# First-stage values in two small tiles by turns, attention's tiles laid out around the first stage, and slots' zeros written in 64 pieces during attention

## The chip, the cores and the metric

The kernel runs on one core of a Trainium2 chip. The metric is the device time of one execution in microseconds (us), here the median of a few runs. TensorE is called PE in the profile (its weight loads PEld), VectorE DVE, ScalarE ACT, GpSimd POOL and SyncE SP; "SPq" and "ACTq" are the sequencers that issue DMAs. All work is in fp32.

## The reference, cut to what matters

Two layers work on an image tensor of 4 x 384 x 32 x 32. What is computed around the change is the first half of layer 0, and where layer 1 needs zeros:

```
x = x + conv0(ln_c(x))          # conv0 is attention with relative positions
    qkv = xt @ w_qkv            # 4096 tokens x 384 -> 3 x 384, 8 heads of 48
    attn = q k^T * s + sk[dy, dx] + sq[dy, dx];  softmax over 1024 keys
    out  = attn v + (attn summed by offset) table_v;  out @ w_proj + b_proj
t = t + ffn0(ln(t))
x = x + conv1(ln_c(x))          # depthwise convolutions, 7 x 7
t = t + moe(ln(t))              # 4 experts, the 2 best of each token
```

For the experts the kernel sorts token rows into an array of slots in device memory, `xs_d`: 4 experts x 4096 slots of 384 numbers, 25.2 MB. Slots that no token fills must hold zeros, so the whole array is zeroed before the tokens' rows are scattered into it.

## The kernel before, in words

The program has three phases, one after the other in the source: `qkv_phase` (the first stage), `attention_phase` and `rest_phase`. A scheduler orders the instructions of each engine; instructions that are marked `keep_in_program_order` (`pin`, and the helpers `mm`, `dma`, `bulk`, lines 223 to 235) keep their written order among themselves. Tiles of on-chip memory are taken from pools (named groups of buffers). When a pool is closed, its bytes are free for the next pools, and an instruction that writes a tile over freed bytes first waits until the earlier users of those bytes are done.

**First stage** (lines 133 to 202). The 4096 tokens come in 8 blocks of 512, `t` = 0 to 7. `load(t)` fetches the block `xt` on SP's queue; line 160 fetches the weights `wq`. `token_stats` (lines 78 to 98) transposes the block on PE with the matrix `ident` (line 87) and takes mean and variance on DVE; `center` (lines 121 to 130) subtracts the mean over input rows from the weights, once, with the matmuls of line 128. `ident` itself is made at the very start by `make_identity` (line 1501; a memset and an affine select on POOL, shown as masks.py:197 and masks.py:199). For each block PE makes the per-token scale (line 117), six products of q and k rows (36 matmuls, line 175), the next block's statistics and four products of value rows (24 matmuls, line 186). DVE scales each q or k product into one of four buffers `qk_sb` (line 179), and POOL's queue writes it to device memory, `qk_d` (line 180). ACT scales the value products into `va` (line 189), one tile for all 8 blocks, zeroed in one POOL memset (line 147); POOL's queue writes each block's part to `v_d` (line 194). In blocks 2 to 5 POOL's queue also writes the zeros of `xs_d`, two transfers of 3072 KB per block, from a tile `zero` of one row (lines 198 to 202).

**Attention** (lines 205 to 651). Small loads come first: the tables `tab`, q and k of head 0 as `kq` (lines 273 to 285), keys `kk`. For each of 8 heads `prepare` (lines 298 to 324) makes two tables of position terms: 32 pairs of matmuls `tabq_ps` and `tabk_ps`; DVE transposes each `tabk_ps` into the tile `b2` (line 318), ACT copies each `tabq_ps` into `st` (line 322), and SP's queue writes `st` to device memory, `sd`. Then come 32 rows `y` of the image (lines 565 to 639), for all 4 images at once. The row loop is a software pipeline written out by hand. For row `y` it issues, on SP's queue, `queries` for two rows ahead (line 568, even `y`), `fetch(blk[y + 3])` (line 570: a load of `s1` out of `sd`, 240 KB, then POOL additions at line 353 that make the tile `bias`), and one piece of the head's value table `tvw` (`next(pieces)`, line 574, 192 KB). DVE adds `bias` to the scores (line 381) two rows ahead, ACT takes exponentials (line 391), PE transposes (line 410) and, every fourth row, multiplies with the values `vb` (line 440, `av_ps`). From `y` = 19 on ACT's queue loads the next head's `kq` (line 576). All waits run through buffers: three of `s1`, three of `bias`, two of `qs`, two score buffers `sc_ps`.

**Layout.** The pools of the first stage and those of attention start at the same byte of each partition, behind the pool `held`. Within a pool tiles lie in the order in which they are written down. The first stage has `va` (65,536 bytes per partition), `zero` (1,536), `wq` (13,824), then three `xt` (18,432), the small tiles, two `scale` (4,096), `s_dg` (2,048) and four `qk_sb` (8,192). Attention's pool `a_fixed` has `b2` (61,440), three pairs of `arow` and `extra` (18,432), two `den` (256), then `vb` (8,192), `aT` (16,384), `a1t` (32,768), `tvs` (1,024), `tvw` (24,576); the working tiles (`st`, `bias`, `s1`, `oT`, `qs`) lie behind these, past the first stage's last byte.

**Rest** (from line 894): projection, feed-forward, convolution, gates, scatter into `xs_d` (line 1205), experts. Its first scatter runs 1763.6 us into the span.

Of the kernel before, what the change touches and what calls it, by code (L numbers as in the profile page):

```python
# [11 lines left out]
F32 = mybir.dt.float32  # L12
# [6 lines left out]
P = 128  # L19
B, C, IMG = 4, 384, 32  # L20
# [3 lines left out]
HEADS, HD = 8, C // 8  # L24
# [4 lines left out]
NBLK = N // P  # L29
PADR = 6  # L30
AROWS = IMG + 2 * PADR
YB = 4
YT = 16
XT = 8
VW = 64
# [3 lines left out]
NEXP = 4  # L39
TOK = 512  # L40
# [6 lines left out]
CAP = B * N  # L47
# [23 lines left out]
def bcast(ap, dim, n):  # L71

    dims = [list(d) for d in ap.ap]
    dims[dim] = [0, n]
    return bass.AP(ap.tensor, ap.offset, dims)
# [25 lines left out]
def result(steps):  # L101

    while True:
        try:
            next(steps)
        except StopIteration as end:
            return end.value
# [13 lines left out]
def center(nc, psum, tag, one, w):  # L121

    n = w.shape[2]
    for c in range(0, n, C):
        part = w[:, :, c : min(c + C, n)]
        ps = psum.tile([P, part.shape[2]], F32, tag=tag, name="sum_ps")
        for k in range(KC):
            nc.tensor.matmul(ps, one, part[:, k, :], start=(k == 0), stop=(k == KC - 1))
        for k in range(KC):
            nc.vector.scalar_tensor_tensor(part[:, k, :], ps, -1.0 / C, part[:, k, :], ALU.mult, ALU.add)  # L130


def qkv_phase(tc, cst, x, w_qkv, qk_d, v_d, xs_d):

    nc = tc.nc
    one, ident = cst["one"], cst["ident"]
    with ExitStack() as es:  # L140
        wp = es.enter_context(tc.tile_pool(name="q_w", bufs=1))
        work = es.enter_context(tc.tile_pool(name="q_work", bufs=2))
        ev = es.enter_context(tc.tile_pool(name="q_ev", bufs=4))
        psum = es.enter_context(tc.tile_pool(name="q_ps", bufs=3, space=PSUM))
        psmm = es.enter_context(tc.tile_pool(name="q_mm", bufs=4, space=PSUM))
        va = wp.tile([P, HEADS, B * NBLK, VW], F32, name="va")
        nc.gpsimd.memset(va, 0.0)
        zero = wp.tile([P, 1, C], F32, name="zero")
        nc.gpsimd.memset(zero, 0.0)
        wq = wp.tile([P, KC, 3 * C], F32, name="wq")  # L150
        xts = {}

        def load(t):
            b, n0 = divmod(t * TOK, N)
            xts[t] = work.tile([P, KC, TOK], F32, tag="xt", name="xt", bufs=3)
            nc.sync.dma_start(xts[t], x[b, :, n0 : n0 + TOK].rearrange("(k p) n -> p k n", p=P))

        load(0)
        for k in range(KC):
            nc.sync.dma_start(wq[:, k, :], w_qkv[k * P : (k + 1) * P, :])  # L160
        stats = result(token_stats(nc, (work, psum, "st"), ident, xts[0], cst["eps6"]))
        center(nc, psum, "st", one, wq)
        for t in range(NT // TOK):
            b, n0 = divmod(t * TOK, N)
            xt = xts.pop(t)
            _, rstd = stats
            ps = to_partitions(nc, (work, psum, "st"), ident, one, rstd)
            scale = work.tile([P, TOK], F32, tag="scale", name="scale")
            nc.scalar.copy(scale, ps)
            if t + 1 < NT // TOK:  # L170
                load(t + 1)
            for m in range(2 * KC):
                ps = psmm.tile([P, TOK], F32, tag="mm", name="qk_ps")
                for k in range(KC):
                    nc.tensor.matmul(
                        ps, wq[:, k, m * P : (m + 1) * P], xt[:, k, :], start=(k == 0), stop=(k == KC - 1)
                    )
                sb = ev.tile([P, TOK], F32, tag="qk", name="qk_sb")
                nc.vector.tensor_tensor(sb, ps, scale, ALU.mult)
                nc.gpsimd.dma_start(qk_d[m * P : (m + 1) * P, t * TOK : (t + 1) * TOK], sb)  # L180
            if t + 1 < NT // TOK:
                stats = result(token_stats(nc, (work, psum, "st"), ident, xts[t + 1], cst["eps6"]))
            for j in range(TOK // P):
                ps = psmm.tile([P, TOK], F32, tag="mm", name="v_ps")
                for k in range(KC):
                    nc.tensor.matmul(
                        ps[:, :C], xt[:, k, j * P : (j + 1) * P], wq[:, k, 2 * C :], start=(k == 0), stop=(k == KC - 1)
                    )
                nc.scalar.activation(
                    va[:, :, t * (TOK // P) + j, :HD], ps[:, :C].rearrange("p (h d) -> p h d", d=HD),  # L190
                    AF.Copy, scale=rstd[:, j, :],
                )
            w = NBLK // 2 * VW
            nc.gpsimd.dma_start(
                v_d.rearrange("h p n -> p h n")[:, :, t * w : (t + 1) * w],
                va[:, :, t * NBLK // 2 : (t + 1) * NBLK // 2, :].rearrange("p h c d -> p h (c d)"),
            )
            if 2 <= t < 2 + NEXP:
                rows = xs_d[(t - 2) * CAP : (t - 1) * CAP].rearrange("(n p) c -> p n c", p=P)
                n = rows.shape[1] // 2  # L200
                for r in (rows[:, :n], rows[:, n:]):
                    tc.keep_in_program_order(nc.gpsimd.dma_start(r, bcast(zero, 1, r.shape[1])))


def attention_phase(tc, cst, held, tabs, tv, qk_d, v_d, ao_d, heads):

# [12 lines left out]
    nc = tc.nc  # L221
# [15 lines left out]
    with ExitStack() as es:  # L237
        dram = es.enter_context(tc.tile_pool(name="a_dram", bufs=2, space=DRAM))
        fixed = es.enter_context(tc.tile_pool(name="a_fixed", bufs=1))
# [4 lines left out]
        ps_o = es.enter_context(tc.tile_pool(name="a_ps_o", bufs=1, space=PSUM))  # L244

        ident = cst["ident"]
        b2 = fixed.tile([P, SPAN, IMG, IMG], F32, name="b2")

        NA = 3
        arow, extra = [], []  # L250
        for i in range(NA):
            a = fixed.tile([P, AROWS, IMG], F32, name=f"arow{i}")
            nc.gpsimd.memset(a, 0.0)
            arow.append(a)
            x = fixed.tile([P, 4, IMG], F32, name=f"extra{i}")
            nc.gpsimd.memset(x, 0.0)
            extra.append(x)
        den = []
        for i in range(2):
            d = fixed.tile([P, IMG], F32, name=f"den{i}")  # L260
# [2 lines left out]


        kq, kk, tab = held
        vb = fixed.tile([P, B, NBLK, VW], F32, name="vb")
        aT = fixed.tile([P, NBLK, YB, P], F32, name="aT")
        a1t = fixed.tile([P, 4, IMG, YT, B], F32, name="a1t")
        tvs = fixed.tile([64 + HD, B // 2, YT, XT], F32, name="tvs")
        nc.gpsimd.memset(tvs, 0.0)  # L270
        tvw = fixed.tile([P, 4, IMG, HD], F32, name="tvw")

        def load_tables(h, bulk=bulk):
            for lo, i, r0 in ((64, 0, h * HD), (0, 1, C + h * HD)):
# [246 lines left out]
                yield  # L521


        batch, o = None, None

        def new_head(h):
            sd = dram.tile([P, IMG, SPAN * IMG], F32, tag="sd", name="sd")
# [8 lines left out]
        for n, h in enumerate(heads):  # L536
# [28 lines left out]
            for y in range(IMG):  # L565
                s, r = blk[y], y % YT
# [5 lines left out]
                    add_aside(batch[1], 3)  # L572
                if y:
                    next(pieces, None)
                if y >= YT + 3:
                    next(loads, None)
                if batch and r in (3, 7):
# [917 lines left out]
@with_exitstack  # L1495
def metaformer_kernel(ctx: ExitStack, tc: tile.TileContext, ins, out):
    nc = tc.nc
    cp = ctx.enter_context(tc.tile_pool(name="const", bufs=1))
    dram = ctx.enter_context(tc.tile_pool(name="scratch", bufs=1, space=DRAM))
    ident = cp.tile([P, P], F32, name="ident")  # L1500
    make_identity(nc, ident)
    one = cp.tile([P, P], F32, name="one")
    nc.vector.memset(one, 1.0)
    cst = {"ident": ident, "one": one}
    for name, v in (("eps5", 1e-5), ("eps6", 1e-6)):
        t = cp.tile([P, 1], F32, name=name)
        nc.vector.memset(t, v)
        cst[name] = t
    qk_d = dram.tile([2 * C, NT], F32, name="qk_d")
    v_d = dram.tile([HEADS, P, B * NBLK * VW], F32, name="v_d")  # L1510
    ao_d = [dram.tile([C, B, YT * IMG], F32, name=f"ao_d{i}") for i in range(2)]
    x2_d = dram.tile([C, NT], F32, name="x2_d")
    xs_d = dram.tile([NEXP * CAP, C], F32, name="xs_d")
    y_d = dram.tile([ALL * BLK, C], F32, name="y_d")

    with tc.tile_pool(name="held", bufs=1) as pool:
        held = [
            pool.tile([64 + HD, *n], F32, name=name)
            for name, n in (("kq", [NT]), ("kk", [B, N // 2]), ("tab", [SPAN, ZW]))
        ]  # L1520
        qkv_phase(tc, cst, ins["x"], ins["w_qkv"], qk_d, v_d, xs_d)
        attention_phase(tc, cst, held, ins["tabs"], ins["tv"], qk_d, v_d, ao_d, list(range(HEADS)))
    rest_phase(tc, cst, ins["x"], ao_d, ins, xs_d, y_d, x2_d, out)


# [69 lines left out]
```

## Time and profile before

| What | Value |
|---|---|
| runs | 3087.72 us, median of 3 (3082.57 to 3088.3) |
| profiled execution | 3092.57 us |
| its span, first to last instruction | 3090.6 us |
| mean granted PE clock in it | 0.976 of full |
| PE busy | 2929.9 us (95%) |
| first position table of head 0 (`tabq_ps`) starts | 237.46 us |
| last PE instruction of attention ends | 1507.8 us |
| transfers `xs_d<-zero`, 8 of 3072 KB, issued | 102.7 to 205.6 us |

A waits line reads: the engine and its instruction that stood idle, what ended the wait, the sum in us, the number of times, the longest. A timeline line reads: start in us, duration in us, engine, line, operation, out<-in, shape, count, and in brackets the engine's idle time before it and what ended it. A windows line gives, for a stretch of the span, each engine's busy us and instructions, the granted PE clock (PEclk), the share of the 16 DMA engines that were busy and the GB/s that they moved.

### The profile page before, as it was taken

What the parts mean: (1) busy time and instruction counts of PE and PEld (TensorE: products, weight loads), DVE (VectorE), ACT (ScalarE), POOL (GpSimd) and SP (SyncE); (2) the same over time, 40 slices, a digit from 0 to 9 for tenths busy, and PEclk for the clock granted to TensorE, in tenths of its full rate; (3) what the DMA queues carried; (4) which work ended last, traced back from release to release, by engine and by line L of the source; (5) the groups of instructions that cost most, each with busy time, mean ns of one, the idle gap of its engine ahead of it and who ended that gap; (6) DMA issues with size and microseconds to landing.
All of it is one profiled execution on the core that took longest, in us unless ns stands there. A gap on an engine that the chain in (4) does not pass through costs nothing.

```text
span 3090.6 us, 63376 instructions
## 1 busy us (share of the span) xinstructions
PE 2929.9 (95%) x25391; PEld 2020.6 (65%) x25391; DVE 1956.6 (63%) x3575; ACT 1370.8 (44%) x2833; POOL 1170.7 (38%) x1132
## 2 busy tenths in 40 slices
PE   8997999999999999999899789999999989999996
PEld 4544676777677677776533347776577867777775
DVE  2226787878787877777568869999899640001101
ACT  1104666666767666666322232333342243233332
POOL 3223747473747473737400122252124231124412
PEclk9998999999999999999999879999999999999998
DMA  3796565656565656564500314734243065366742
GB/s 123 259 320 212 130 203 131 206 132 203 134 202 134 200 131 196 136 199 128 186 21 34 128 31 156 274 136 154 75 175 132 26 229 215 134 227 250 263 180 72
DMA packets 262791, 500.55 MB, mean 162 GB/s; under 512 B 134736, under 2 KB 186832, under 8 KB 254816
## 3 DMA queue, kind: packets, MB, share of 16 engines
q1 hardware_dynamic: 169168, 247.12, 26.0%
q0 software_dynamic: 43424, 227.84, 20.0%
q10 hardware_dynamic: 49904, 21.53, 3.6%
q8 instruction: 200, 3.28, 0.5%
q14 instruction: 95, 0.78, 0.1%
HBM read 543.58 MB, written 152.37 MB: 225 GB/s over the span
## 4 chain that ended last, share of the span: by engine, by line
PE 67%; DVE 13%; issue 11%; POOL 4%; DMA 3%; ACT 2%; another core or an unknown queue 0%; SPq 0%; POOLq 0%; DVEq 0%; ACTq 0%
PE e_ps L1301 12%; PE y_ps L1279 12%; DVE xb L1089 8%; PE t_ps L410 7%; PE av_ps L227 7%; PE sc_ps L227 7%; PE tabq_ps L227 5%; PE a_ps L420 3%; PE tv_ps L227 2%; PE proj_ps L977 2%; PE tabk_ps L227 1%; PE tap_ps L1137 1%; DVE extra L402 1%; PE f_ps L1012 1%; PE o_ps L1016 1%
## 5 line engine op out<-in xcount | busy, mean ns | idle before, releaser
L1301 PEld LDWEIGHTS e_ps<-xT,w 128*128 128x128 f32 x4824 | 656.5, 193 | 217.7 <-issue 14.6
L353 POOL TENSOR_TENSOR bias<-b,s 128x416 f32<-128x416 f32 (+24 forms) x656 | 659.2, 1042 | 178.1 <-DMA s<-sd 157.5
L1301 PE MATMUL e_ps<-xT,w 128*128 128x128 f32 x4824 | 670.6, 277 | 14.1 <-DVE xb L1030 5.0
L1279 PE MATMUL y_ps<-w,eh 128*128 128x384 f32 x1608 | 651.9, 490 | 17.2 <-ACT eh L1304 14.8
L1089 DVE SCALAR_TENSOR_TENSOR xb<-img,pack,xb 128x1024 f32<-128x1024 f32 (+1 forms) x539 | 634.7, 1241 | 0.0
L1304 ACT ACTIVATE eh<-e_ps,w 128x128 f32<-128x128 f32 x804 | 292.9, 367 | 725.3 <-PE e_ps L1301 669.5
L1269 POOL DMA_INDIRECT w<-in_w,row x134 | 171.4, 1279 | 749.7 <-PE y_ps L1279 301.4
L402 DVE TENSOR_REDUCE extra<-arow 128x32 f32<-128x32 f32 (+24 forms) x768 | 381.3, 555 | 9.4 <-ACT arow L391 5.7
L381 DVE CUSTOM_DVE_ANT_0 arow<-sc_ps,bias 128x1024 f32<-128x1024 f32 x256 | 312.5, 1221 | 107.1 <-issue 55.5
L410 PEld LDWEIGHTS t_ps<-ident,arow 128*128 128x128 f32 x2048 | 221.2, 142 | 175.9 <-ACT aT L411 100.6
L391 ACT ACTIVATE arow<-arow,nm 128x1024 f32<-128x1024 f32 x256 | 302.4, 1181 | 70.8 <-DVE nm L381 70.8
L411 ACT COPY aT<-t_ps 128x512 f32<-128x512 f32 x512 | 278.6, 603 | 95.3 <-PE t_ps L410 95.0
L410 PE MATMUL t_ps<-ident,arow 128*128 128x128 f32 x2048 | 283.2, 282 | 17.1 <-ACT arow L391 17.0
L1282 DVE TENSOR_TENSOR yo<-y_ps,w 128x384 f32<-128x384 f32 x67 | 37.0, 553 | 396.0 <-PE y_ps L1279 387.8
L227 PE MATMUL sc_ps<-kk,qs 48*32 48x512 f32 x4096 | 279.2, 608 | 7.7 <-DVE nm L381 6.7
L1279 PEld LDWEIGHTS y_ps<-w,eh 128*128 128x128 f32 x1608 | 248.3, 193 | 31.9 <-ACT eh L1304 19.4
L227 PEld LDWEIGHTS av_ps<-aT,vb 128*64 128x64 f32 x4096 | 222.3, 137 | 52.0 <-ACT aT L411 40.4
L227 PE MATMUL av_ps<-aT,vb 128*64 128x128 f32 x4096 | 237.7, 274 | 0.0
L318 DVE STREAM_TRANSPOSE b<-tabk_ps 128x480 f32<-128x480 f32 x256 | 218.4, 983 | 23.5 <-PE tabk_ps L227 22.2
L227 PE MATMUL tabk_ps<-tab,kq 48*128 48x480 f32 x512 | 223.0, 582 | 6.1 <-DVE b L318 6.1
L227 PE MATMUL tabq_ps<-tab,kq 48*128 48x480 f32 x512 | 220.1, 579 | 2.1 <-ACT aT L411 1.4
L322 ACT COPY st<-tabq_ps 128x480 f32<-128x480 f32 x256 | 142.3, 560 | 71.0 <-PE tabk_ps L227 45.0
(211 smaller groups left out, 3163.4 us busy)
## 6 DMA issues: line engine op xcount, KB each, us to landing
sd<-st SPq DMA_DIRECT2D x128, 480.0 KB
s<-sd SPq DMA_DIRECT2D x256, 240.0 KB
xs_d<-zero POOLq DMA_DIRECT2D x8, 3072.0 KB
tvw<-in_tv SPq DMA_DIRECT2D x120, 192.0 KB
y_d<-yo SPq DMA_DIRECT2D x67, 192.0 KB
qk_d<-qk_sb POOLq DMA_DIRECT2D x48, 256.0 KB
qs<-qk_d SPq DMA_DIRECT2D x256, 48.0 KB
kq<-qk_d ACTq DMA_DIRECT2D x56, 192.0 KB
```

The lines of the kernel that those rows point to most:

```text
L227: ins = nc.tensor.matmul(*args, **kw)
L318: turn = nc.vector.transpose(b2.rearrange("p e y x -> p x (e y)")[:, i + j], ps[:, j, : SPAN * IMG])
L353: nc.gpsimd.tensor_tensor(bias[:, y0:y1, :], bass.AP(b2.tensor, b2.offset + (e * IMG + y0) * IMG, [list(b2.ap[0]), [(step * IMG + 1) * IMG ...
L381: nc.vector.tensor_tensor_reduce(s["flat"], ps.rearrange("p h n -> p (h n)"), s["bias"].rearrange("p y x -> p (y x)"), -SCALE, BIG, ALU.ad ...
L391: nc.scalar.activation(s["flat"], s["flat"], AF.Exp, bias=s["nm"], scale=-1.0, accum_out=dn[:, y % YT : y % YT + 1])
L402: pin(nc.vector.tensor_reduce(ex[:, i, :], a[:, p0:p1, :].rearrange("p y x -> p x y"), AX.X, ALU.add))
L410: pin(nc.tensor.transpose(pt[:, j, :], s["flat"][:, k0 : k0 + P], ident))
L411: pin(nc.scalar.copy(aT[:, 4 * g : 4 * g + 4, s["y"] % YB, :], pt))
L1089: ins_ = nc.vector.scalar_tensor_tensor(acc[:, k, y0:y1], img[:, k, dy + y0 : dy + y1, dx : dx + IMG], w7[:, k, dy, dx : dx + 1], acc[:, k ...
L1279: nc.tensor.matmul(py, hs, w[:, o : o + C], start=(ff == 0), stop=(ff == NF - 1))
L1301: nc.tensor.matmul(ph, w[:, o : o + P], xT[k][:, c, :], start=(c == 0), stop=(c == KC - 1))
L1304: nc.scalar.activation(hs, ph, AF.Gelu, bias=w[:, o : o + 1])
```

## The change

- `va` of the first stage becomes two tiles `va0` and `va1` of 8,192 bytes per partition, one block each, used by turns (`vas[t % 2]`). They are zeroed by DVE, not POOL.
- The tile `zero` and the writes of zeros into `xs_d` leave the first stage.
- In `attention_phase` the tiles `vb`, `aT`, `a1t` and `tvw` are written down first, ahead of `b2`; so they take the first 81,920 bytes, and `b2`, `arow`, `extra`, `den` and `tvs` lie behind them. A tile `zero` (1,536 bytes, POOL memset) joins them.
- A generator `clear` issues one write of 256 rows of zeros (384 KB) per step on SP's queue, pinned in order; the row loop steps it at `y` = 6, 9, 12, 15, 18, 21, 24 and 27 of each head, after that row's `fetch` and `tvw` piece and ahead of ACT's load for that row. 8 steps by 8 heads make the 64 pieces.

```
-def qkv_phase(tc, cst, x, w_qkv, qk_d, v_d, xs_d):
+def qkv_phase(tc, cst, x, w_qkv, qk_d, v_d):
...
-        va = wp.tile([P, HEADS, B * NBLK, VW], F32, name="va")
-        nc.gpsimd.memset(va, 0.0)
-        zero = wp.tile([P, 1, C], F32, name="zero")
-        nc.gpsimd.memset(zero, 0.0)
+        vas = [wp.tile([P, HEADS, TOK // P, VW], F32, name=f"va{i}") for i in range(2)]
+        for va in vas:
+            nc.vector.memset(va, 0.0)
...
                 nc.scalar.activation(
-                    va[:, :, t * (TOK // P) + j, :HD], ps[:, :C].rearrange("p (h d) -> p h d", d=HD),
+                    vas[t % 2][:, :, j, :HD], ps[:, :C].rearrange("p (h d) -> p h d", d=HD),
...
-                va[:, :, t * NBLK // 2 : (t + 1) * NBLK // 2, :].rearrange("p h c d -> p h (c d)"),
+                vas[t % 2].rearrange("p h c d -> p h (c d)"),
             )
-            if 2 <= t < 2 + NEXP:
-                rows = xs_d[(t - 2) * CAP : (t - 1) * CAP].rearrange("(n p) c -> p n c", p=P)
-                n = rows.shape[1] // 2
-                for r in (rows[:, :n], rows[:, n:]):
-                    tc.keep_in_program_order(nc.gpsimd.dma_start(r, bcast(zero, 1, r.shape[1])))
...
-def attention_phase(tc, cst, held, tabs, tv, qk_d, v_d, ao_d, heads):
+def attention_phase(tc, cst, held, tabs, tv, qk_d, v_d, ao_d, xs_d, heads):
...
         ident = cst["ident"]
+        vb = fixed.tile([P, B, NBLK, VW], F32, name="vb")
+        aT = fixed.tile([P, NBLK, YB, P], F32, name="aT")
+        a1t = fixed.tile([P, 4, IMG, YT, B], F32, name="a1t")
+        tvw = fixed.tile([P, 4, IMG, HD], F32, name="tvw")
         b2 = fixed.tile([P, SPAN, IMG, IMG], F32, name="b2")
...
+        zero = fixed.tile([P, 1, C], F32, name="zero")
+        nc.gpsimd.memset(zero, 0.0)
...
-        vb = fixed.tile([P, B, NBLK, VW], F32, name="vb")
-        aT = fixed.tile([P, NBLK, YB, P], F32, name="aT")
-        a1t = fixed.tile([P, 4, IMG, YT, B], F32, name="a1t")
         tvs = fixed.tile([64 + HD, B // 2, YT, XT], F32, name="tvs")
         nc.gpsimd.memset(tvs, 0.0)
-        tvw = fixed.tile([P, 4, IMG, HD], F32, name="tvw")
...
+        def clear():
+
+            rows = 2 * P
+            for n0 in range(0, NEXP * CAP, rows):
+                dma(
+                    xs_d[n0 : n0 + rows].rearrange("(n p) c -> p n c", p=P), bcast(zero, 1, rows // P),
+                )
+                yield
+
         batch, o = None, None
+        cleared = clear()
...
                 if y:
                     next(pieces, None)
+                if 6 <= y < 30 and y % 3 == 0:
+                    next(cleared)
                 if y >= YT + 3:
                     next(loads, None)
```

More of the change, by code (lines that the diff above doesn't have):

```diff
@@ L1520, in metaformer_kernel @@
         ]
-        qkv_phase(tc, cst, ins["x"], ins["w_qkv"], qk_d, v_d, xs_d)
-        attention_phase(tc, cst, held, ins["tabs"], ins["tv"], qk_d, v_d, ao_d, list(range(HEADS)))
+        qkv_phase(tc, cst, ins["x"], ins["w_qkv"], qk_d, v_d)
+        attention_phase(tc, cst, held, ins["tabs"], ins["tv"], qk_d, v_d, ao_d, xs_d, list(range(HEADS)))
     rest_phase(tc, cst, ins["x"], ao_d, ins, xs_d, y_d, x2_d, out)
```

## The prediction

> **What bounds the kernel now.** I read the page's busy times, then the waits and the timeline of the first stage, then the boundary to attention, then the waits of attention's rows.
>
> ```profile
> PE 2929.9 (95%) x25391; PEld 2020.6 (65%) x25391; DVE 1956.6 (63%) x3575; ACT 1370.8 (44%) x2833; POOL 1170.7 (38%) x1132
> ```
>
> PE is the bound nearly everywhere, so a gain can only come from stretches in which PE stands still or is slowed. The change touches three of them.
>
> The start (timeline; start, duration, engine):
>
> ```profile
> 0.88 13.76 POOL L147 MEMSET va<- 128x16384 f32 x1
> 3.99 0.49 SPq L232 DMA_DIRECT2D tab<-in_tabs  x1
> 14.68 0.28 POOL masks.py:199 TENSOR_SCALAR_AFFINE_SELECT ident<-ident 128x128 f32<-128x128 f32 x1
> ...
> 15.02 2.82 PE L87 MATMUL row_ps<-ident,xt 128*128 128x128 f32 x12 [15.02 <-POOL ident masks.py:199]
> ```
>
> The memset of `va` runs on POOL between the two steps that make `ident`; PE's first instruction waits for `ident`, not for data.
>
> The middle (PE's timeline at line 117, once per block, and the waits of 0 to 240 us):
>
> ```profile
> 100.76 1.02 PE L117 MATMUL all_ps<-s_dg,one 128*128 128x512 f32 x2
> ...
> 126.12 1.02 PE L117 MATMUL all_ps<-s_dg,one 128*128 128x512 f32 x2
> ...
> 151.85 1.02 PE L117 MATMUL all_ps<-s_dg,one 128*128 128x512 f32 x2
> ...
> 184.02 1.02 PE L117 MATMUL all_ps<-s_dg,one 128*128 128x512 f32 x2
> ...
> 210.44 1.02 PE L117 MATMUL all_ps<-s_dg,one 128*128 128x512 f32 x2
> ```
> ```profile
> DVE qk_sb L179 <- DMA qk_d<-qk_sb: 58.7, 10, 14.5
> ...
> PE qk_ps L175 <- DVE qk_sb L179: 7.0, 3, 4.3
> ```
>
> Blocks take 25.36 us each until the zeros come; then 25.73, 32.17 and 26.42. DVE finds its four `qk_sb` still being written out, and PE finds no free bank.
>
> The boundary (timeline):
>
> ```profile
> 237.69 0.90 POOL L194 DMA_DIRECT2D v_d<-va  x1 [7.09 <-ACT va L189]
> ...
> 246.05 0.13 DVE L261 MEMSET den<- 128x32 f32 x2 [16.28 <-DMA kk<-qk_d]
> 246.05 1.27 POOL L253 MEMSET arow<- 128x1408 f32 x1 [7.46 <-DMA sd<-st]
> 246.09 3.44 DVE L318 STREAM_TRANSPOSE b<-tabk_ps 128x480 f32<-128x480 f32 x4
> ```
>
> DVE and POOL start at the same moment, on tiles that lie over the first stage's bytes. The named releasers are only the last in time; what ends here is the last `v_d<-va`, whose packets stop at 244.66 in the trace's packet records. `den` lies over `wq` alone (bytes 79,872 on, by the sizes), whose last reader, PE, was done at 236.8; yet it waits as long, so the freed stretch is handed over whole. `st`, past those bytes, was written from 238.73.
>
> In the rows there is little for a delay to hide behind or to free:
>
> ```profile
> PE t_ps L410 <- ACT arow L391: 8.5, 13, 2.2
> PE sc_ps L227 <- DVE nm L381: 6.7, 10, 1.0
> ```
>
> These are PE's two longest waits of 300 to 1500 us. Starts of the value products (line 440) are 13.80 or 13.81 us apart in all eight heads: PE sets the pace of the rows.
>
> **What the Trainium skill says.** (1) "DMA: Bandwidth & Descriptors", section Queues, rings and completion order: each DMA engine takes descriptors in ring order within a queue and goes round between queues. The trace agrees: `qk_d` writes, behind 3072 KB of zeros in POOL's queue, hold DVE up to 14.5 us. It says too where the zeros go: ahead of fetches in SP's ring. (2) "TensorE: Matmul & The Clock Gate", section What's actually happening: after some 3.4 us of idling the array falls to half clock until it has been busy again. The trace agrees: after the gap at 242 to 248 us `tabk_ps` takes 1.17 us, else 0.56. (3) "VectorE: DVE Perf Modes", section Zero memsets can be issued as uint32: a memset costs a cycle per element. Each new `va` has 2,048 elements, at the 0.96 GHz of "Trainium Kernel Development and Optimization" (NeuronCore Architecture) an estimate of 2.1 us; no DVE memset of that size is in the trace.
>
> **The change part by part.**
>
> *Start.* POOL's 13.76 us go; DVE gets two memsets, 4.3 us, from about 1.0 to 5.3. What is late next is data: the packets of the first `xt` end at 4.86, those of `wq` at 9.06. A landed fetch in attention takes at least 0.5 us to release its reader, so transposes can start at 5.4 and run 2.8 us; the first matmul of line 128 needs all of `wq`, so 9.6 instead of 17.63. From there everything is a PE chain as before. DVE's first statistics come after 5.4, so the memsets are covered; without cover they would cost nothing up to 9.6 either. One `arow` memset (1.27) could slip ahead of `ident` on POOL; still under 4.86. Gain **8.0** (bounds 6.5 to 8.2).
>
> *Middle.* Excess over 25.36: 0.37 + 6.81 + 1.06 = 8.24 for blocks 4 to 6. In block 7 line 117 to the first value product takes 18.44 (210.44 to 228.88), where 36 matmuls leave 16.31 in block 0: 2.13. Without zeros the remaining traffic is that of blocks 0 to 3 (130 to 142 GB/s), which stalled nothing. Eight POOL issues of 1.16 us go too, off the path. Turning two `va` by turns adds a wait of ACT for the `v_d` write two blocks (50 us) earlier: nothing, as that lands within 9. Gain **10.4** (bounds 8.2 to 10.4; the 2.1 us that block 5 loses to a lowered clock belong to the stall).
>
> *Boundary.* The first stage now takes about 63,100 bytes (16,384 + 13,824 + 18,432 + 6,100 + 8,192 + small), less than the 81,920 of `vb`, `aT`, `a1t`, `tvw`; so `b2`, `arow`, `den` meet bytes that nobody used. The first transpose (line 318) can follow the first `tabk_ps` at 238.4, not 246.09: 7.65. Steady spacing is 0.827; the three spacings after the restart were 1.39, 1.60, 1.21, since PE came back at half clock: 1.72 more. What is late next is DVE's own 32 x 0.827. The new sitters wait for the first stage, but are wanted later: `vb` is loaded from 278 and needs `v_d` anyway, `aT` is written at 285. Gain **9.4** (bounds 7.6 to 9.4; nothing if the area is not split as sized).
>
> *Zeros in attention.* 64 x 384 KB. SP's issue: 0.42 us, from `vb<-v_d`. Transfer: 256 rows of 1,536 bytes; such packets (`y_d<-yo`) take 66 ns on one engine, so 256 x 66 / 16 = 1.06 us. Behind a piece at even `y` (6, 12, 18, 24) SP issues the second fetch of the pair at once: rows 10, 16, 22, 28 come up to 1.5 us later. At odd `y` the next thing on SP is `queries`, which waits for PE anyway. The slack of these fetches I added up from the records: from the last packet to POOL's start (less 0.5), DVE's wait from `bias` to line 381, and that result's wait until PE needs the score buffer. The least of 8 heads is 7.1 us for row 10, 1.7 for row 16, 16.3 for row 22, 3.5 for row 28. So all hide; without cover 32 x 1.5 = 48 us. From `y` = 21 on the pieces share the engines with ACT's `kq` loads, so I take **1 us** of loss (bounds 0 to 8). `zero`'s memset (0.4 on POOL) hides. Layout at attention's end: rest's first loads wait for the last `tv_ps` at 1507.9; that stays.
>
> Sum: 8.0 + 10.4 + 9.4 - 1 = 26.8. Against the profiled execution (3092.57, span 3090.6): 3065.8. The median of the runs is 4.85 lower, so 3087.72 - 26.8 = **3061**.
>
> **The rivals.**
> A, the layout does not free `b2`: some first-stage tile or a coarser hand-over still holds DVE until `v_d` has landed. For it: `den` shows hand-over of a whole stretch. Against: `st` did not wait. Without the backlog the wait would also shrink; at worst 8.0 + 10.4 - 1 = 17.4, so 3070.
> B, the rows pay for the zeros. For it: row 16's slack is 1.7 in one head, and DVE waits 40.5 us for `bias`; a piece may take twice 1.06 beside `kq` loads. One mechanism: SP's ring delays `s<-sd`, POOL's additions come late, PE waits for scores. From 27.8 / 64 = 0.43 us exposed per piece it turns the change into a loss; at the full 1.5 on all, 96 - 27.8: slower, 3156; with 0.6 exposed, 3098. Against it: the slacks.
> C, the time is given back at the start: another input (`tab`, `wq`) or the order that the scheduler finds holds PE until about 15. Then 18.8: 3069.
> D, the pieces do not do what is said, or the rest's order shifts so that it cancels: near 3087.
>
> **How the numbers follow.** Forecast 0.80, own range 3053 to 3072 (bounds above: gain 14.3 to 28.0, and 3 us of spread between runs). A 0.08, C 0.05, B 0.04, D 0.03. A measurement can tell some 0.2% from no change. Faster: forecast, A and C, 0.93; slower 0.04; same 0.03. The range 3052 to 3074 holds the forecast, A and C.
>
> **What would show it.** After: PE's first sum_ps near 9.6; line 117 eight times 25.36 apart; no `DMA qk_d<-qk_sb` wait of DVE; the first line 318 within 1 us of the first `tabk_ps`, some 26 us earlier than now; 13.8 us still between value products; head 0 starting its rows 27 to 28 us earlier, and the end of attention about as much. If the value products spread apart around `y` = 12 to 24, B is right; if line 318 still starts with a landing DMA, A.

## The result, and the profile after

The changed kernel takes **3070.02 us**, median of 5 runs (3065.37 to 3077.61), beside 3087.72 for the kernel before on the same chip: 17.7 us less, ratio 0.9948 with a 95% interval of 0.9934 to 0.9963. Run again on two chips beside the experiments, it gave 0.9948 (0.9935 to 0.9961) and 0.9952 (0.9935 to 0.997). The forecast was 3061: the direction is right, the time lies in the range, and about a third of the forecast gain is missing.

The profiled execution of after took 3065.37 us (span 3063.6), 27.2 less than that of before, almost exactly the forecast sum. That agreement is chance. It is the fastest of its five runs. Of the 9.5 us by which these two executions differ more than the medians do, 3.9 come from one gap, between heads 4 and 5, where before's execution stood 29.15 us from one head's last value product to the next head's first (its other gaps 24.7 to 26.7). Such gaps vary from execution to execution of one program: the gap between heads 1 and 2 is 25.38 us in this profile of after and 28.87 in another. What can be compared is the start of the rows, the first value product: 300.96 us before (profiled once), 283.10 after, 283.48 and 282.58 in the two other profiles of the same kernel. The change is worth **17.9 us** there, which is what the medians show.

The page's first line (busy us, share of the span, instructions), then the start (timeline: start, duration, engine):

```profile
PE 2923.0 (95%) x25391; PEld 2018.1 (66%) x25391; DVE 1960.3 (64%) x3577; ACT 1369.9 (45%) x2833; POOL 1150.8 (38%) x1123
```
```profile
1.02 0.29 POOL masks.py:199 TENSOR_SCALAR_AFFINE_SELECT ident<-ident 128x128 f32<-128x128 f32 x1
...
5.36 2.79 PE L87 MATMUL row_ps<-ident,xt 128*128 128x128 f32 x12 [5.36 <-DMA xt<-in_x]
...
7.95 1.70 PE L128 MATMUL sum_ps<-wq,one 128*128 128x384 f32 x3
```

PE works nearly as much as before (2929.9 us busy then, 2923.0 now); most of the gain is idle time. `ident` is ready at 1.3 us instead of 15.0, and PE now waits for data, `xt`, as predicted. Then `sum_ps` follows at 7.95 (17.63 before).

The middle (PE's timeline at line 117):

```profile
90.41 1.02 PE L117 MATMUL all_ps<-s_dg,one 128*128 128x512 f32 x2
115.77 1.02 PE L117 MATMUL all_ps<-s_dg,one 128*128 128x512 f32 x2
141.14 1.02 PE L117 MATMUL all_ps<-s_dg,one 128*128 128x512 f32 x2
166.50 1.02 PE L117 MATMUL all_ps<-s_dg,one 128*128 128x512 f32 x2
191.86 1.02 PE L117 MATMUL all_ps<-s_dg,one 128*128 128x512 f32 x2
```

All blocks are 25.36 us apart, where two of them took 32.17 and 26.42. The wait of DVE for `qk_d<-qk_sb` is gone.

The boundary (timelines of POOL, DVE and PE):

```profile
217.28 0.91 POOL L193 DMA_DIRECT2D v_d<-va  x1 [7.38 <-ACT va L188]
227.46 1.27 POOL L251 MEMSET arow<- 128x1408 f32 x1 [9.28 <-DMA sd<-st]
```
```profile
227.47 0.13 DVE L261 MEMSET den<- 128x32 f32 x2 [18.40 <-DMA sd<-st]
227.51 3.52 DVE L314 STREAM_TRANSPOSE b<-tabk_ps 128x480 f32<-128x480 f32 x4
```
```profile
229.39 1.17 PE L221 MATMUL tabk_ps<-tab,kq 48*128 48x480 f32 x1 [8.23 <-DVE b L314]
```

Nothing changed here but the clock time: DVE and POOL again start at one moment, some 10 us after the last `v_d<-va` was issued, and PE comes back after 8.23 us at half speed (1.17 us a product, else 0.56). As before, the releaser named is only the last event. By the packet records, the last packets of `v_d` end at 226.17 us.

In the rows (waits of PE alone, 300 to 1480 us: sum, times, longest), PE stays the bound:

```profile
PE t_ps L406 <- ACT arow L387: 6.7, 14, 1.5
PE sc_ps L221 <- DVE nm L377: 5.0, 9, 0.8
```

### The profile page after: what moved, and what is told of

It is laid out like the page before. It is cut to its first block, busy times and chain, and to the rows that moved or that the text cites. A ratio compares the mean times of both kernels' runs of the same rounds, so it can differ in the third digit from the quotient of the medians.

```text
span 3063.6 us, 63474 instructions
## 1 busy us (share of the span) xinstructions
PE 2923.0 (95%) x25391; PEld 2018.1 (66%) x25391; DVE 1960.3 (64%) x3577; ACT 1369.9 (45%) x2833; POOL 1150.8 (38%) x1123
## 3 DMA queue, kind: packets, MB, share of 16 engines
q0 software_dynamic: 37792, 202.68, 17.9%
## 4 chain that ended last, share of the span: by engine, by line
PE 74%; DVE 13%; issue 6%; DMA 3%; ACT 2%; POOL 2%; SPq 0%; another core or an unknown queue 0%; DVEq 0%; POOLq 0%; ACTq 0%
PE e_ps L1309 12%; PE y_ps L1287 12%; DVE xb L1097 8%; PE t_ps L406 8%; PE sc_ps L221 7%; PE av_ps L221 7%; PE tabq_ps L221 6%; PE qk_ps L174 4%; PE a_ps L416 4%; PE tv_ps L221 2%; PE v_ps L185 2%; PE proj_ps L985 1%; PE tabk_ps L221 1%; PE tap_ps L1145 1%; PE f_ps L1020 1%
## 5 line engine op out<-in xcount | busy, mean ns | idle before, releaser
L1309 PEld LDWEIGHTS e_ps<-xT,w 128*128 128x128 f32 x4824 | 656.4, 193 | 215.1 <-issue 12.2
L314 DVE STREAM_TRANSPOSE b<-tabk_ps 128x480 f32<-128x480 f32 x256 | 218.5, 982 | 23.7 <-PE tabk_ps L221 22.2
```

Source lines behind the costliest of these rows:

```text
L314: turn = nc.vector.transpose(b2.rearrange("p e y x -> p x (e y)")[:, i + j], ps[:, j, : SPAN * IMG])
L1309: nc.tensor.matmul(ph, w[:, o : o + P], xT[k][:, c, :], start=(c == 0), stop=(c == KC - 1))
```

## The experiments

Each ratio is to the kernel before on the chip of the run. The chips differ: the kernel before takes 3067.71 and 3068.31 us on two, 3083.78 and 3084.49 on two others, and 3087.72 beside the result. So times are compared only within a chip, or as ratios. "The changed kernel" is the one of the result. Two theories for the missing gain stood against each other: the boundary did not open, because a pool takes over freed bytes as one (the theory of the pool), or the zeros' pieces cost something in the rows.

**1. A pool of its own for the tiles over the first stage** (e1_split). Order and, by the sizes, byte addresses stay; `vb`, `aT`, `a1t` and `tvw` come from another pool.

```
+        over = es.enter_context(tc.tile_pool(name="a_over", bufs=1))
         fixed = es.enter_context(tc.tile_pool(name="a_fixed", bufs=1))
...
-        vb = fixed.tile([P, B, NBLK, VW], F32, name="vb")
+        vb = over.tile([P, B, NBLK, VW], F32, name="vb")
...
```

> The changed kernel, but vb, aT, a1t and tvw stand in a pool of their own ahead of a_fixed; every tile keeps its byte address. Theory POOL (a pool takes over its bytes as a whole: one tile over freed bytes makes every tile of that pool wait): den, arow and b2 no longer wait, the first transpose into b2 starts within 1 us of the first tabk_ps instead of 10.5 us later, the clock of PE doesn't fall there, and the median is 9 to 12 us under the changed kernel's 3070, so 3058 to 3061. Theory DATA (the wait at the boundary is for something that b2 really needs, such as the loads of kq or kk): nothing moves, 3070.

Measured: 3039.84 us, ratio 0.9907 (0.9889 to 0.9925), 27.9 us below the kernel before. DVE's timeline at the boundary:

```profile
218.69 7.57 DVE L315 STREAM_TRANSPOSE b<-tabk_ps 128x480 f32<-128x480 f32 x9 [9.14 <-PE tabk_ps L221]
230.46 1.00 DVE L315 STREAM_TRANSPOSE b<-tabk_ps 128x480 f32<-128x480 f32 x1 [4.19 <-PE tabk_ps L221]
```

The transposes now wait for PE's product and start at 218.69, 8.8 us earlier than in after, with `v_d`'s write issued at 217.77, much as in after (217.28); `den` is even set at 5.26 us, long before the first stage ends. Nothing but the pool was changed, so the shared pool was the wait. A part is given back: after nine transposes DVE stands 4.19 us, since ACT finds its three `st` still being written out. By the packet records these writes begin at 224.24, as the load of `kk` ends (223.92) and while `v_d` is still being written (to 226.97). The waits of 216 to 258 us:

```profile
ACT st L319 <- DMA sd<-st: 5.3, 2, 4.8
```

The 32nd transpose ends 4.3 us earlier than in after, the first value product comes 6.8 earlier. One expectation failed: PE's clock still falls (0.60 granted from 231 to 236 us), only later, after this gap.

**2. The old order of tiles** (e7_oldlay): `vb`, `aT`, `a1t`, `tvw` again where they stood in the kernel before, in the one pool.

```
         ident = cst["ident"]
-        vb = fixed.tile([P, B, NBLK, VW], F32, name="vb")
...
         b2 = fixed.tile([P, SPAN, IMG, IMG], F32, name="b2")
...
+        vb = fixed.tile([P, B, NBLK, VW], F32, name="vb")
...
```

> The changed kernel with vb, aT, a1t and tvw written down where they stood before, so that b2 and arow lie over the first stage's bytes again (b2 over va, xt; den now past them). Theory (a pool takes over freed bytes as a whole, so the order of tiles inside it decides nothing): same as the changed kernel within 2 us; the first transpose of tabk_ps still starts about 10 us after the first tabk_ps. Rival (each tile waits for its own bytes only, and the new order was of some use): the transposes begin still later or the time is 3 us or more above the changed kernel.

Measured: 3066.28 us, beside 3068.72 for the changed kernel on the same chip; ratio 0.9945 (0.9932 to 0.9958).

```profile
227.59 0.12 DVE L257 MEMSET den<- 128x32 f32 x2 [18.25 <-DMA sd<-st]
227.64 3.49 DVE L314 STREAM_TRANSPOSE b<-tabk_ps 128x480 f32<-128x480 f32 x4
```

The first transpose starts at the same time whichever tile lies where (227.51 in after). The layout part of the change does nothing that shows.

**3. Only the small tiles, in the kernel before** (e2_start): `va` as two tiles zeroed by DVE; zeros and layout as before.

```
-        va = wp.tile([P, HEADS, B * NBLK, VW], F32, name="va")
-        nc.gpsimd.memset(va, 0.0)
+        vas = [wp.tile([P, HEADS, TOK // P, VW], F32, name=f"va{i}") for i in range(2)]
+        for va in vas:
+            nc.vector.memset(va, 0.0)
...
```

> The kernel before, with one part of the change: two small va by turns, zeroed by DVE; the zeros stay in the first stage and attention's tiles where they were. Theory START (the POOL memset ahead of ident alone held PE at the start): PE starts at 5.4 instead of 15.0, about 10 us are gained and kept, 3077 to 3079; blocks 4 to 7 still lose about 10 us to the zeros. Theory GIVEN BACK (the backlog of the zeros or the last v_d write sets the time of attention's start, so that an earlier start only waits longer): within 2 us of 3088.

Measured: 3062.74 us, ratio 0.9983 (0.9975 to 0.999), 5.0 below the kernel before. The gain shrinks on its way: 8.7 us at line 117, 8.3 at the first `tabq_ps`, 5.9 at the first transpose, 5.0 at the first value product. So neither theory holds as stated: PE does start 9 us earlier, and little more than half of that is kept. Most of the loss lies between the first `tabq_ps` and the first transpose, where the last `v_d` write lands later (see the boundary below).

**4. The zeros back in the first stage** (e6_first): the changed kernel with the eight transfers of 3072 KB on POOL's queue and no pieces.

```
+        zero = wp.tile([P, 1, C], F32, name="zero")
+        nc.vector.memset(zero, 0.0)
...
+            if 2 <= t < 2 + NEXP:
...
+                    tc.keep_in_program_order(nc.gpsimd.dma_start(r, bcast(zero, 1, r.shape[1])))
...
-                if 6 <= y < 30 and y % 3 == 0:
-                    next(cleared)
```

> The changed kernel, with the zeros written in the first stage again (8 transfers of 3072 KB on POOL's queue in blocks 2 to 5), so no pieces during attention. Theory: the stalls of blocks 5 to 7 come back in full, since v_d, qk_d and the zeros share one queue, and the boundary still waits for the last v_d write; first tabq_ps 8 to 11 us later than in the changed kernel, first value product 8 to 12 later, and the rows run at the same pace of 13.8 us with or without the pieces: 8 to 12 us above the changed kernel. Rival (the pieces in attention cost a few us in the rows, hidden so far by noise): from the first value product to the end of attention this kernel is 3 to 8 us faster, so it ends only 2 to 7 us above.

Measured: 3079.78 us, ratio 0.9982 (0.9974 to 0.999), 11.1 above the changed kernel on the same chip. The waits of 0 to 240 us:

```profile
DVE qk_sb L180 <- DMA qk_d<-qk_sb: 59.3, 9, 14.7
...
DVE den L268 <- DMA sd<-st: 18.4, 1, 18.4
```

DVE's stall is back as it was before (58.7 us in 10 waits), and the first `tabq_ps` comes 11.1 us later than in the changed kernel. Of these 0.4 lie at the start (line 117 first at 15.08, not 14.66), the rest in the middle. Between the first and the last value product of a head both kernels take the same time within 0.2 us, so the pieces cost the rows nothing that shows.

This kernel is 4.7 us below the kernel before, much as experiment 3's is 5.0 below. By parts, then, the small tiles are worth about 5 us, moving the zeros about 11, and the new order of tiles nothing.

**5. Roomier places for the pieces** (e8_roomy).

```
-                if 6 <= y < 30 and y % 3 == 0:
+                if y in (6, 10, 14, 15, 16, 17, 18, 22):
```

> The changed kernel with the eight pieces per head at y = 6, 10, 14, 15, 16, 17, 18, 22 in place of 6, 9, ... 27: behind them come fetches of rows with at least 7 us of slack. Theory (a single piece of some 1.5 us fits into the slack wherever it stands): same as the changed kernel within 3 us. Rival (the pieces at y = 12 and 24, ahead of rows 16 and 28 with least slacks of 1.7 and 3.5 us, are paid for): 3 to 10 us below the changed kernel, gained inside the heads.

Measured: 3069.67 us, 1 above the changed kernel (3068.72); ratio 0.9948 (0.9935 to 0.9962). The pieces ahead of rows 16 and 28 cost nothing that shows: from the first to the last value product each head takes as long as in the changed kernel's profile on this chip (r_after), within 0.2 us.

**6. Each piece written twice** (e3_double).

```
-                dma(
+                for _ in range(2):
+                    dma(
...
```

> The changed kernel, with every piece of zeros written twice (128 pieces of 384 KB in attention). Theory HIDDEN (the slack of the fetches hides a piece): within 2 us of the changed kernel, 3070, value products still 13.8 us apart. Theory ROWS PAY (each piece on SP's queue makes rows late): the 64 more pieces cost 0.1 to 1.5 us each, 3076 to 3166. Two pieces delay the next fetch by up to 3 us, more than the least slack of 1.7 us counted for row 16, so a few us at that row would fit HIDDEN with the slack as I counted it.

Measured: 3121.65 us, ratio 1.0174 (1.0153 to 1.0196). Read alone this would make the zeros' traffic dear. The waits say otherwise: SP's queue, then PE, 300 to 1530 us:

```profile
SPq L226 <- DMA xs_d<-zero: 292.7, 61, 7.0
```
```profile
PE sc_ps L221 <- DVE nm L377: 33.1, 31, 3.1
PE t_ps L406 <- ACT aT L407: 18.2, 7, 3.1
```

The second write goes to the rows of the first, so SP waited for that one to land, 4.8 us on average, with all row fetches queued behind it. The experiment added a wait beside the traffic, and does not tell the two apart.

**7. Two pieces far apart** (e10_twofar): the same doubled traffic, without that wait.

```
-                dma(
+                for r0 in (n0, (n0 + NEXP * CAP // 2) % (NEXP * CAP)):
+                    dma(
...
```

> The changed kernel with two pieces at each place, 12.6 MB apart (piece n and piece n + 32, round the array's end), so every row is zeroed twice but no piece waits for the one just issued: twice the traffic of zeros, without the 292.7 us that SP waited for landings in e3_double. Theory (the pieces' transfers fit into the rows' slack; e3_double paid for a wait of its own making): 0 to 15 us above the changed kernel, SP waits for landing zeros under 30 us. Rival (the traffic itself is what the rows pay for): 50 us or more above the changed kernel, as e3_double.

Measured: 3075.18 us, ratio 0.997 (0.996 to 0.998). The changed kernel's ratio is 0.9948, so this is 0.0022 x 3084 = 6.8 us above it. The intervals touch, so the size is rough; inside the heads, from the first to the last value product, the profile shows 5.0 us more than r_after's. SP's longest waits no longer name the zeros:

```profile
SPq L226 <- ACT st L318: 224.1, 112, 8.3
SPq L226 <- PE t_ps L406: 187.7, 47, 11.9
SPq L226 <- PE sc_ps L221: 78.9, 54, 3.6
```

Sixty-four more pieces cost about 7 us, 0.1 us each; a few groups of four rows are stretched (15.42, 14.85 and 14.35 us in place of 13.81), most are not. Experiment 6 stood 69 us above the changed kernel by the ratios; what it lost beyond these 7 goes with the wait, which went when the second piece was written elsewhere.

**8. The pieces early in the head** (e4_early): two different pieces at each of `y` = 1 to 4.

```
-                if 6 <= y < 30 and y % 3 == 0:
+                if y in (1, 2, 3, 4):
+                    next(cleared)
                     next(cleared)
```

> The changed kernel, with its 64 pieces moved to the rows where the slack was least: two pieces at each of y = 1, 2, 3 and 4 of every head. Theory SLACK (a piece costs what it exceeds the slack of the fetch behind it): rows 3 to 6 have 0.7 to 3.9 us and get 3 us of delay, so PE waits some 2 to 6 us per head, 3085 to 3115, and all of it before the value products of y = 8. Theory FREE (a piece in SP's ring never costs anything, since DMA engines are idle a third of the time): 3070.

Measured: 3074.11 us, ratio 1.0019 (1.0011 to 1.0028), 0.7% or some 20 us above the changed kernel by the ratios, and slower than the kernel before. The same 64 pieces cost nothing at `y` = 6 to 27 and more than the whole gain at 1 to 4. In every head it is the first group of four rows that is stretched (14.19, 13.95 and 17.93 us, not 13.81, in heads 0 to 2), as SLACK said. From the first value product of a head to the last it loses 0.2 to 4.2 us against a profile of the changed kernel (r_after2), 17 in the eight heads. DVE's wait for `bias`, 240 to 1500 us:

```profile
DVE arow L377 <- POOL bias L349: 94.4, 55, 7.7
```

In r_after2 the same wait is 57.6 us in 33, and PE's wait for scores (`sc_ps` for `nm`) is 7.8 us there, 22.2 here: late fetches reach PE on the way that rival B named. Added up as for the prediction, rows 3 and 5 have 0.7 us of slack in their tightest head. That two pieces stand at one place is not enough to explain the loss: experiment 7 has two at each of its 64 places and loses 5.0 us inside the heads.

**9. The engine that zeroes** (e11_pool): the two small `va` zeroed by POOL.

```
-            nc.vector.memset(va, 0.0)
+            nc.gpsimd.memset(va, 0.0)
```

> The changed kernel with the two small va zeroed by POOL, not DVE: two memsets of about 13.76 / 8 = 1.72 us between the two steps that make ident, which is then ready near 4.7. Theory (what counts is that ident is ready before xt has landed, whatever engine zeroes): PE's first transpose stays at 5.4 and the time within 2 us of the changed kernel. Rival (it is the engine that counts): the first transpose at 6 or later, and the time up by as much.

Measured: 3066.67 us, ratio 0.9944 (0.993 to 0.9958). PE's start, then POOL's:

```profile
5.53 2.79 PE L87 MATMUL row_ps<-ident,xt 128*128 128x128 f32 x12 [5.53 <-DMA xt<-in_x]
```
```profile
0.88 1.81 POOL L148 MEMSET va<- 128x2048 f32 x1
2.74 0.28 POOL masks.py:199 TENSOR_SCALAR_AFFINE_SELECT ident<-ident 128x128 f32<-128x128 f32 x1
2.97 1.79 POOL L148 MEMSET va<- 128x2048 f32 x1
```

One memset still comes between the two steps of `ident`, but a short one: `ident` is there at 3.0, before `xt`. The size of the tile made the start late, not the engine.

**10. The own pool beside the changed kernel** (e9_split2, r_after2; r_after is the changed kernel on the chip of experiments 2, 4 and 5).

> The kernel of e1_split once more (the changed kernel, with vb, aT, a1t and tvw in a pool of their own), now with the changed kernel on the same chip. Theory: the transposes of tabk_ps start 1.4 us after the first tabk_ps, the first value product comes 6.5 to 7.5 us earlier than in the changed kernel, and that is the whole gain: 5 to 9 us below the changed kernel, 22 to 27 below the kernel before. Rival: the other pool layout frees more than the first transposes (stalls between the heads too); then 10 us or more below the changed kernel, as the two ratios taken on different chips suggest.

> The changed kernel again, as the neighbour of the run before: 15 to 18 us below the kernel before, first value product near 283 us.

> The changed kernel itself, on the chip of the following runs, as their anchor. If its structural gain is the 10.4 us at the start plus 10.4 in the middle less about 2 to 3 at the boundary, it stands 17 to 19 us below the kernel before here too, and its rows begin (first value product) 17 to 18 us earlier. If the 27 us between the two profiled executions is the true gain, it stands 24 to 28 below.

Measured: r_after 3068.72 us, 15.8 below the kernel before; r_after2 3052.02 us, ratio 0.9952; e9_split2 **3039.79** us, ratio 0.9918 (0.9901 to 0.9935). So the version with its own pool is 12.2 us below the changed kernel on one chip, and the fastest of all. The rival was right that it frees more than the first transposes, though not where it said. The first value product comes 7.0 us earlier, the rows keep that. The rest lies at the end of attention (SP's queue: a wait and the timeline in the changed kernel, then the timeline with the own pool):

```profile
SPq L972 <- PE tv_ps L221: 7.3, 1, 7.3
```
```profile
1489.13 0.38 SPq L972 DMA_DIRECT2D at<-ao_d  x1
```
```profile
1469.64 0.47 SPq L973 DMA_DIRECT2D at<-ao_d  x1
```

The last `tv_ps` ends at 1488.97 and at 1476.78. In the changed kernel the rest's first load starts right after it, having waited for it; with two pools that wait is gone and the load is issued 7.1 us ahead of it. The last `tv_ps` reads `a1t` and `tvw`, which are in the other pool now; so here too it was the one pool, handed over whole, that held the load. From the last `tv_ps` to the first `proj_ps` it is then 4.11 us, not 6.95, and the first `f_ps` comes another 1.2 sooner: 4.0 in all. (From the last `tv_ps` to `f_ps` it is 31.8 and 32.2 us in the two profiles of this kernel, 34.7 to 36.3 in all others.) With 7.0 that is 11.0 of the 12.2; the remainder, and 5 us that the two profiles differ by between heads, are within what one kernel's executions differ by.

## Why the prediction was right in its direction, and where its sum was wrong

*Start*, forecast 8.0, measured 10.35 (line 117 of block 0 at 24.67 before, 14.32 after; 14.66 in another execution): right mechanism, size off. Two terms. The step "the first matmul of line 128 needs all of `wq`, so 9.6" failed: `wq` is loaded in three transfers and each product needs one of them, so PE began at 7.95 with the first; 9.68 us instead of 8.0. The other 0.67 came between there and line 117 (7.04 us before, 6.37 after); the first three `sum_ps` alone took 2.13 us before and 1.70 after. Why was not tested; the profiles of the changed kernel and of the experiments with its first stage have 6.2 to 6.8 us there, so part of it is one execution. The memsets on DVE were covered, as said:

```profile
1.40 1.76 DVE L148 MEMSET va<- 128x2048 f32 x1 [0.38 <-issue]
...
3.54 1.76 DVE L148 MEMSET va<- 128x2048 f32 x1 [0.38 <-issue]
```

Each is busy for 1.76 us, but with the gap before it they follow each other by 2.14 us and end at 5.30, as forecast: the estimate of 2.1 us from "VectorE: DVE Perf Modes" fits that pace. Experiments 3 and 9 show that it is the tile's size that gives this gain.

*Middle*, forecast 10.4, measured 20.71 - 10.35 = 10.36 by the first `tabq_ps`: right. Experiment 4 puts the stall back and loses 11.1.

*Boundary*, forecast 9.4, measured -2.9 (20.71 gained at the first `tabq_ps`, 17.86 at the first value product; -1.1 to -3.3 by the other profiles with one pool): **the failed step**. It was "`b2`, `arow`, `den` meet bytes that nobody used. The first transpose (line 318) can follow the first `tabk_ps`". They do meet unused bytes, and it did not follow. Within the pool `a_fixed` the hand-over knows no tiles: a part of the pool lies over the first stage, and the tiles that are written first, `den`, `arow` and `b2`, all wait for the first stage's last `v_d` write, wherever they lie. (So "an instruction that writes a tile over freed bytes", in the description of the kernel above, has to read: a tile of a pool any part of which lies over freed bytes.) Experiment 1 parts the pool and the wait is gone; experiment 2 changes the order inside it and nothing happens. The evidence lay in the profile of before: `den` lay over `wq` alone and waited as long, which the prediction read as "the freed stretch is handed over whole". Its counter-example, `st`, which did not wait, is from another pool (`a_work`), and that was overlooked; it showed where the border runs. Rival A stated this case and gave it 0.08.

Of the -2.9, some 2 us lie between the first `tabq_ps` and `den` (8.6 us before, 10.7 after): the last `v_d` packets end 6.97 us after their issue before and 8.9 after. Experiments 3 and 4 lose 2.1 to 2.4 there as well, though they hold the zeros of before; so it comes with the small tiles or the early start, not with the zeros. By the packet records the delay lies ahead of the first packet, 1.9 us after the issue before and 3.2 to 3.8 in every run with small tiles. Why was not settled. Had the step held, it would have been worth 4.5 to 4.7 rather than 9.4: from the first `tabq_ps` to the first value product it is 63.50 us before, 66.35 after, and 59.05 and 58.83 with the own pool. The prediction took DVE's own transposes for the next bound, and it was `st`, whose writes come behind the load of `kk` and the `v_d` write.

*Zeros in attention*, forecast -1: right. Experiments 4 and 5 find no cost; 7 prices 64 more pieces at some 7 us. The single transfer was put at 1.06 us by packets alone; issue to landing takes 4.3 us (median, in r_after2) when it shares the engines. The pace of 13.8 us between value products, which the prediction gives for whole heads, holds for five of the seven steps of a head; the fourth and the last are 21.6 and 39.6, before and after alike. "DMA: Bandwidth & Descriptors" (Queues, rings and completion order) was read rightly: what stands ahead in SP's ring delays what stands behind (experiment 8). But a wait on SP costs more than bytes there: 69 us in experiment 6, 7 in experiment 7. Rival B was wrong for these places, though its mechanism is real: experiment 8 is that rival, and ends slower than before.

*Attention's end*, forecast "that stays": it stayed, in the changed kernel; experiment 10 shows that it need not.

Sum: 10.35 + 10.36 - 2.85 - 0 = 17.86, where the forecast had 26.8. The boundary is 12.25 too high, the start 2.35 too low, the zeros 1 too low. Rival A's 3070 meets the measured median because its own errors cancel: it too had the start 2.35 and the zeros 1 too low, and no loss at the boundary. That the time fell into the stated range is luck as well. The terms' bounds (gain 14.3 to 28.0) and 3 us of spread give 3057 to 3076, not the 3053 to 3072 that was stated, and both the start (6.5 to 8.2) and the boundary (7.6 to 9.4) came out beyond their own.

## What to carry to other kernels

Where tiles are laid over freed bytes, find out at which grain they are handed over before counting on a byte map: here one late write under a pool made all its early tiles wait, while a pool of their own for the tiles that really overlap takes one more line and was worth 12 us, at both ends of attention. If two tiles in a trace behave differently, look for everything in which they differ, not only for the property that suits the plan. A doubling experiment must not add a dependence: read the waits of the experiment before its time.

## What was not expected of the hardware

One program runs at different speeds on different chips: 3067.71 and 3068.31 us on two, 3083.78 and 3084.49 on two others, for the kernel before. In the profiles, the difference lies behind the first scatter, in the part with the experts: from there to the end 1305 to 1308 us on the first two chips, 1318 to 1327 in all other profiles, whichever of these kernels ran. The cause was not looked for.
